# Layer 0 of a four-layer network: 64x64 quadrants for the queries and the attention results, and the values' product moved next to the keys' product

## The chip, the cores and the metric

The program runs on one core of one Trainium2 chip. The metric is the device time of one execution in microseconds (us), and less is better. Everything is computed in fp32.

## The reference, cut to what matters

The network has four layers on an input of 2 x 512 x 32 x 32. Only layer 0, a deformable attention with eight heads of 64 channels, is touched by the change. Cut to the steps that the change and the prediction speak of, it computes:

```python
xn = bn(x)
q = gconv1x1(xn, qw)                     # eight groups of 64 channels, each with its own 64x64 matrix
off = conv(q, off_dw_w, stride 4)        # 6x6 depthwise, padded by 1
...                                      # gelu, tanh: 64 sampling positions for each head
kv = grid_sample(xn, positions)
k = gconv1x1(kv, kw)
v = gconv1x1(kv, vw)
bias = mlp(log-distance of each of 1024 queries to each of 64 positions)   # 2 -> 128 -> 128 -> 1
attn = softmax(q k^T / 8 + bias)
out = attn v                             # 1024 queries x 64 channels for each head
x = x + out_w out + out_b                # then an MLP, and layers 1 to 3
```

The costly part is `mlp` of the bias: 2 images x 8 heads x 64 positions x 1024 queries go through a 128 x 128 matrix.

## The kernel before, in words

**Units.** A head of one image is a *unit* `u` (16 of them). Two heads lie in one tile of 128 channels and make a *pair* (8 pairs). Each unit is cut into 8 steps `o` of two halves `jj`: 16 *quads* for each unit, 256 in all. A quad covers four positions of a head against all 1024 queries.

**The work of a quad.** `first_hidden` (L436) makes the first hidden layer on DVE: four instructions of L445, each 128 x 1024, into two tiles `h1` of a pool of four, so that the quad after next waits until the quad before it has been read. `second_hidden` (L456) makes on PE 4 x 2 x 4 products of 128 x 32 weights (L476, four of them side by side in the four column groups), in four PSUM tiles `hp` of two banks each from the pool `ps` (three such tiles, taken in turn). ACT evicts each `hp` with a ReLU (L481) and scales some (L483, L487), POOL scales and adds (L485, L492, L494) and issues accumulating DMAs (L468). `last_product` (L498, L508) folds two finished quads into `sim`. Every second quad starts with one DVE instruction that makes the table `y` in the PSUM tile `bank` (L433).

**The work behind the quads.** Two generators are advanced by one step after each quad. `front` is `offsets` (L257) and `sampled` (L326) of the next pair. `after` is `attend` (L516) of a finished unit. Their steps that matter here are these:

- `offsets`: L264 makes `xn`; L271 multiplies it by the queries' weights, two products of 128 x 128 by 128 x 512. The weight tile holds the two heads' 64 x 64 matrices on its diagonal and zeros elsewhere. The result `q` takes one tile of `ps`. L274 copies it on ACT into the middle of a 34 x 34 padded image `qpad`. Then DVE makes the depthwise convolution: six products L278 (three in one step, three in the next) and a reduction L291, and so on to the positions.
- `sampled`: the sampled `kv`, then the keys' product (L379) into `bank`, two DVE instructions that scale the keys (L382), the values' product (L384) into another part of `bank`, and its copies to two halves of `v` on DVE (L386) and ACT (L387).
- `attend`: keys by queries into `sim` (L523), DVE's L531, four transposes (L535), the softmax (L540 to L547, the exponential L543 on ACT), four transposes back (L551), a copy (L555), and the product of the values with the attention (L564): two products of 64 x 64 weights by 64 x 512, one for each half of the queries, with the halves' 64 positions in different rows of the array and the results in the same 64 columns. ACT copies the result, 64 x 1024, to `att` (L567). The last unit has no tile of `ps` left and uses `bank` and `sim`, with one copy on ACT (L569) and one on DVE (L570).

**What sets the order.** PE, ACT, DVE and POOL take their instructions strictly in the order in which this code emits them (`manual_schedule`); nothing is reordered. The waits between the engines come from the tiles that they share. In one turn of the loop the code emits the next quad's `first_hidden`, then this quad's `second_hidden`, then one step of `after`, then one step of `front`.

Of the kernel before, what the change touches and what calls it, by code (L numbers as in the profile page):

```python
# [11 lines left out]
F32 = mybir.dt.float32  # L12
# [6 lines left out]
P = 128  # L19
B, C, H, W = 2, 512, 32, 32  # L20
N = H * W
CT = C // P
NB = N // P
HF = 512
DH = 64
NJ = 64
# [21 lines left out]
class Net:  # L48
# [208 lines left out]
    def offsets(self, m, bt, ps):  # L257

        nc = self.nc
        b, t = divmod(bt, CT)
        xn = m["xn"] = self.fone.tile([P, N], F32, tag="xn", name=f"xn{b}{t}")
        nc.vector.tensor_scalar(xn, self.xs[b][t], self.s1[:, t : t + 1], self.col("bn1_b", t), ALU.mult, ALU.add)  # L264
        qp = m["q"] = self.fpool.tile([P, HP, HP], F32, tag="qpad", name=f"qpad{b}{t}")
        for edge in (qp[:, 0, :], qp[:, HP - 1, :], qp[:, :, 0], qp[:, :, HP - 1]):
            nc.gpsimd.memset(edge, 0.0)
        yield
        q = ps.tile([P, 2, HF], F32, tag="ps", name=f"q{b}{t}")
        for h in range(2):  # L270
            nc.tensor.matmul(  # L271
                q[:, h, :], lhsT=self.l0qkv[:, 0, t, :], rhs=xn[:, h * HF : (h + 1) * HF], start=True, stop=True
            )
        nc.scalar.copy(qp[:, 1 : 1 + H, 1 : 1 + W], q.rearrange("p h (r w) -> p (h r) w", w=W))  # L274
        yield
        prod = self.fone.tile([P, 6, 6, NJ], F32, tag="prod", name=f"prod{b}{t}")
        for ky in range(6):
            nc.vector.tensor_tensor(  # L278
                prod[:, ky, :, :].rearrange("p k (y x) -> p k y x", y=8),
                bass.AP(  # L280
                    tensor=qp.tensor,
                    offset=qp[:, ky, 0:1].offset,
                    ap=[list(qp.ap[0]), [1, 6], [4 * HP, 8], [4, 8]],
                ),
                self.colr("dw_w", len(TAPS))[:, 6 * ky : 6 * ky + 6].unsqueeze(2).unsqueeze(3).to_broadcast([P, 6, 8, 8]),
                ALU.mult,
            )
            if ky % 3 == 2:
                yield
        conv = self.fpool.tile([P, NJ], F32, tag="conv", name=f"conv{b}{t}")  # L290
        nc.vector.tensor_reduce(conv, prod.rearrange("p a b j -> p j (a b)"), AX.X, ALU.add)  # L291
        yield
        ge = self.fpool.tile([P, NJ], F32, tag="ge", name=f"ge{b}{t}")
        nc.scalar.activation(ge, conv, AF.Gelu, bias=self.col("dw_b"))
        yield
        o = self.bank[:, 256:258]
        for par in range(2):
            rows = slice(par * DH, (par + 1) * DH)
            nc.tensor.matmul(o[rows, :], lhsT=ge[rows, :], rhs=self.colr("pw", 2)[rows, :], start=True, stop=True)
        at = self.fpool.tile([P, 2], F32, tag="at", name=f"at{b}{t}")  # L300
        nc.scalar.activation(at, o, AF.Tanh)
        yield
        nc.vector.scalar_tensor_tensor(at, at, 4.0, self.grid[:, G_KEY : G_KEY + 2], ALU.mult, ALU.add)
        nc.vector.tensor_scalar(at, at, 2.0 / 7.0, -1.0, ALU.mult, ALU.add)
        pos = self.fpool.tile([P, 2, W], F32, tag="pos", name=f"pos{b}{t}")
        nc.vector.tensor_tensor(
            pos,
            self.grid[:, G_QRY : G_QRY + W].unsqueeze(1).to_broadcast([P, 2, W]),
            at.unsqueeze(2).to_broadcast([P, 2, W]),
            ALU.subtract,  # L310
        )
        yield
        log = self.fpool.tile([P, 2, W], F32, tag="log", name=f"log{b}{t}")
        nc.scalar.activation(log, pos, AF.Abs)
        nc.scalar.activation(log, log, AF.Ln, bias=1.0)
        nc.scalar.activation(pos, pos, AF.Sign)
        yield
        nc.vector.tensor_tensor(log, log, pos, ALU.mult)
        logs = self.dram.tile([P, 2 * W], F32, tag="logs", name=f"logs{b}{t}")
        nc.sync.dma_start(logs, log.rearrange("p d x -> p (d x)"))  # L320
        spots = self.dram.tile([P, 2], F32, tag="spots", name=f"spots{b}{t}")
        nc.sync.dma_start(spots, at)
        m["log"], m["logs"], m["spots"] = log, logs, spots
        yield

    def sampled(self, m, bt, ps):  # L326
# [3 lines left out]
        nc = self.nc  # L330
        b, t = divmod(bt, CT)
        xn = m["xn"]
        g = self.fone.tile([P, 2, 2 * NJ], F32, tag="g", name=f"g{b}{t}")
# [12 lines left out]
        w = self.fone.tile([P, NB, 2 * NJ], F32, tag="w", name=f"w{b}{t}")  # L346
# [16 lines left out]
        for n in range(NB):  # L363
            for par in range(2):
                rows = slice(par * DH, (par + 1) * DH)
                nc.tensor.matmul(
                    kv_ps[rows, :],
                    lhsT=xnT[:, n, rows],
                    rhs=w[:, n, rows],
                    start=(n == 0),  # L370
                    stop=(n == NB - 1),
# [5 lines left out]
        yield  # L377
        k_ps = self.bank[:, 448:512]
        nc.tensor.matmul(k_ps, lhsT=self.l0qkv[:, 1, t, :], rhs=kv, start=True, stop=True)  # L379
        for par in range(2):  # L380
            rows = slice(par * DH, (par + 1) * DH)
            nc.vector.tensor_scalar(keys[rows, par, :], k_ps[rows, :], DH**-0.5, None, ALU.mult)  # L382
        v_ps = self.bank[0:NJ, 256:384]
        nc.tensor.matmul(v_ps, lhsT=kv, rhs=self.l0qkv[:, 2, t, :], start=True, stop=True)  # L384
        vals = self.fpool.tile([P, P], F32, tag="v", name=f"v{b}{t}")
        nc.vector.tensor_copy(vals[0:NJ, :], v_ps)  # L386
        nc.scalar.copy(vals[NJ:P, :], v_ps)  # L387
# [128 lines left out]
    def attend(self, u, m, sim, att, ps):  # L516
        nc = self.nc
        g = u % 8
        rows = slice((g % 2) * DH, (g % 2 + 1) * DH)
        for h in range(2):  # L520
            for jj in range(2):
                at = h * NJ + jj * 32
                nc.tensor.matmul(  # L523
                    sim[at : at + 32, :],
                    lhsT=m["k"][:, g % 2, jj * 32 : jj * 32 + 32],
                    rhs=m["q"][:, 1 + 16 * h : 17 + 16 * h, 1 : 1 + W],
                    start=False,
                    stop=True,
                )
        ss = self.soft.tile([P, HF], F32, tag="ss", name=f"ss{u}")  # L530
        nc.vector.tensor_scalar(ss, sim, self.col("cpb_b3"), None, ALU.add)  # L531
        yield
        tp = ps.tile([P, 8, NJ], F32, tag="ps", name=f"tp{u}") if ps else self.bank.rearrange("p (a j) -> p a j", j=NJ)
        for i in range(4):
            nc.tensor.transpose(  # L535
                tp[:, 2 * i : 2 * i + 2, :].rearrange("p a j -> p (a j)"), ss[:, i * P : (i + 1) * P], self.ident
            )
        st = self.soft.tile([P, 3, 8], F32, tag="st", name=f"st{u}")
        e = self.soft.tile([P, 8, NJ], F32, tag="e", name=f"e{u}")
        nc.vector.tensor_reduce(st[:, 0, :], tp, AX.X, ALU.max)  # L540
        nc.vector.tensor_tensor(e, tp, st[:, 0, :].unsqueeze(2).to_broadcast([P, 8, NJ]), ALU.subtract)
        yield
        nc.scalar.activation(e, e, AF.Exp)  # L543
        yield
        nc.vector.tensor_reduce(st[:, 1, :], e, AX.X, ALU.add)
        nc.vector.reciprocal(st[:, 2, :], st[:, 1, :])
        nc.vector.tensor_tensor(e, e, st[:, 2, :].unsqueeze(2).to_broadcast([P, 8, NJ]), ALU.mult)  # L547
        yield
        pp = ps.tile([P, HF], F32, tag="ps", name=f"pp{u}") if ps else self.bank
        for i in range(4):  # L550
            nc.tensor.transpose(  # L551
                pp[:, i * P : (i + 1) * P], e[:, 2 * i : 2 * i + 2, :].rearrange("p a j -> p (a j)"), self.ident
            )
        pt = self.soft.tile([P, HF], F32, tag="pt", name=f"pt{u}")
        nc.vector.tensor_copy(pt, pp)  # L555
        yield
        if ps:
            o = ps.tile([P, N], F32, tag="ps", name=f"o{u}")
            parts = [o[:, h * HF : (h + 1) * HF] for h in range(2)]
        else:  # L560
            parts = [self.bank, sim]
        for h, part in enumerate(parts):
            half = slice(h * NJ, (h + 1) * NJ)
            nc.tensor.matmul(part[rows, :], lhsT=m["v"][half, rows], rhs=pt[half, :], start=True, stop=True)  # L564
        to = att[g // 2]
        if ps:
            nc.scalar.copy(to[rows, :], o[rows, :])  # L567
        else:
            nc.scalar.copy(to[rows, 0:HF], self.bank[rows, :])  # L569
            nc.vector.tensor_copy(to[rows, HF:N], sim[rows, :])  # L570
        yield

    def project(self, ps, att, w, bias: str, b: int):
# [652 lines left out]
```

## Time and profile before

| | |
|---|---|
| time, three runs | 3575.72, 3578.60, 3578.97 us; median 3578.6 |
| the profiled execution | 3578.05 us, span of its instructions 3576.3 us |
| PE busy | 3497.6 us of the span |
| DVE, ACT, POOL busy | 2023.0, 1976.3, 1869.8 us |
| layer 0 | the first 2106 us, of which the first 36 us are a start without quads |
| L476, all quads | 16384 records in 1825.1 us |

An fp32 product shows as two records of PE, and a record's end is modelled. Four records of different quadrants or column groups run side by side, so that a quad's 64 records take 16 places of 0.43 us. A busy PE therefore does not say that PE never waits: while one column group waits for its data, the records around it still count as busy. The chain of waits shows such places better. In the views that follow, the first number of a timeline or chain row is its start in us, the second how long it lasts.

### The profile page before, as it was taken

Reading aid. Unit: us, or ns where it says so; the run is one execution under the profiler, and the core shown is the slowest. Engines: PE = TensorE matmul, PEld = TensorE weight load, DVE = VectorE, ACT = ScalarE, POOL = GpSimd, SP = SyncE. Lnnn points to the kernel's source line nnn. Section 1 sums busy time; section 2 is a strip of 40 time slices with the busy share of each in tenths; the row PEclk is TensorE's granted clock in tenths of the full one; section 3 lists DMA queues with packets and bytes.
Section 4 is the critical chain, followed back from the end, with each engine's and each line's share of the span. In section 5 each row is a group of like instructions: output and inputs, shape, how many; then the busy total and the mean of one; then the engine's idle time right before and its main releaser. Section 6 shows DMA issues by size and latency. Waiting matters only on the chain.

```text
span 3576.3 us, 58840 instructions
## 1 busy us (share of the span) xinstructions
PE 3497.6 (98%) x25184; PEld 1248.3 (35%) x25184; DVE 2023.0 (57%) x2075; ACT 1976.3 (55%) x2003; POOL 1869.8 (52%) x1392
## 2 busy tenths in 40 slices
PE   7999999999999999999999999999999999999998
PEld 2322332332323332332333334444644333443333
DVE  6877777767767668768766620000242467423674
ACT  5877787877776677777777720011010465102661
POOL 4878777787786687887788810000011344012441
PEclk9999999999999999999999999999999999999999
DMA  5777777787786687787888740000000000000001
GB/s 154 152 144 154 153 152 146 151 162 144 153 160 120 125 161 145 151 159 145 167 163 161 146 162 0 0 0 0 1 3 0 36 1 3 15 0 1 1 1 48
DMA packets 101799, 334.70 MB, mean 94 GB/s; under 512 B 12561, under 2 KB 14225, under 8 KB 100241
## 3 DMA queue, kind: packets, MB, share of 16 engines
q0 software_dynamic: 73296, 266.90, 39.4%
q1 hardware_dynamic: 27216, 61.82, 5.6%
q8 instruction: 202, 3.31, 0.4%
q10 hardware_dynamic: 1008, 2.06, 0.2%
q14 instruction: 77, 0.62, 0.1%
HBM read 59.40 MB, written 4.46 MB: 18 GB/s over the span
## 4 chain that ended last, share of the span: by engine, by line
PE 94%; DVE 5%; issue 1%; ACT 0%; POOL 0%; DMA 0%; DVEq 0%; ACTq 0%
PE hp L476 47%; PE m L619 6%; PE m L628 6%; PE s L956 6%; PE o L985 6%; PE qk0p L848 3%; PE pb L585 3%; PE qk1p L848 3%; PE sim L508 3%; PE vp L889 3%; DVE h L445 2%; DVE prod L278 1%; PE out_b L585 1%; PE d L1002 1%; DVE conv L291 1%; PE ob L193 1%
## 5 line engine op out<-in xcount | busy, mean ns | idle before, releaser
L476 PE MATMUL hp<-h,w 128*32 128x512 f32 x16384 | 1825.1, 593 | 7.4 <-DVE h L445 5.9
L445 DVE CUSTOM_DVE_ANT_1 h<-tx,bank 128x1024 f32<-128x1024 f32 x1024 | 1180.9, 1215 | 344.8 <-PE hp L476 321.7
L481 ACT ACTIVATE h<-hp,magb 128x1024 f32<-128x1024 f32 x1024 | 1123.7, 1112 | 437.1 <-PE hp L476 436.1
L476 PEld LDWEIGHTS hp<-h,w 128*32 128x32 f32 x16384 | 529.6, 110 | 1233.2 <-issue 1151.6
L468 POOL DMA_DIRECT2D h<-h x509 | 452.7, 1026 | 406.7 <-ACT h L487 348.5
L494 POOL TENSOR_TENSOR h<-h,h 128x1024 f32<-128x1024 f32 x255 | 614.6, 2410 | 21.3
L492 POOL TENSOR_SCALAR h<-h,flip 128x1024 f32<-128x1024 f32 x256 | 448.9, 1754 | 0.9 <-ACT h L481 0.9
L960 ACT ACTIVATE e<-s 128x1024 f32<-128x1024 f32 x256 | 258.7, 1024 | 152.7 <-PE s L956 152.6
L483 ACT ACTIVATE h<-h,flip 128x1024 f32<-128x1024 f32 x256 | 291.3, 1138 | 0.0
L956 PE MATMUL s<-q,k 64*64 64x512 f32 x2048 | 259.9, 590 | 5.1 <-ACT e L960 3.4
L985 PE MATMUL o<-e,v 64*64 64x512 f32 x2048 | 260.8, 592 | 0.0
L659 POOL MEMSET l1ones<- 128x128 f32 x1 | 0.2, 205 | 476.0 <-PE m L628 476.0
L623 ACT ACTIVATE mh<-m,cols 128x512 f32<-128x512 f32 x64 | 44.0, 687 | 336.5 <-PE m L619 336.5
L619 PE MATMUL m<-mx,w 128*128 128x512 f32 x512 | 220.5, 592 | 0.9 <-issue 0.9
L628 PE MATMUL m<-mh,w 128*128 128x512 f32 x512 | 220.4, 592 | 0.0
L967 POOL TENSOR_TENSOR some<-some,e 128x1024 f32<-128x1024 f32 x64 | 151.3, 2364 | 82.5 <-ACT e L960 80.0
L636 DVE SCALAR_TENSOR_TENSOR x<-m,cols,x 128x512 f32<-128x512 f32 x16 | 12.0, 750 | 318.0 <-PE m L628 318.0
L485 POOL TENSOR_SCALAR h<-h,flip 128x1024 f32<-128x1024 f32 x128 | 154.5, 1207 | 64.0 <-ACT h L481 62.8
L965 POOL TENSOR_TENSOR some<-e,e 128x1024 f32<-128x1024 f32 x32 | 75.9, 2371 | 212.6 <-ACT q L994 139.2
L862 POOL TENSOR_TENSOR sq<-q 128x1024 f32<-128x1024 f32 x16 | 30.3, 1894 | 280.3 <-DVE q L856 280.3
L860 ACT ACTIVATE k<-qk1p,cols 128x512 f32<-128x512 f32 x32 | 22.0, 687 | 245.0 <-PE qk1p L848 245.0
L487 ACT ACTIVATE h<-h,flip 128x1024 f32<-128x1024 f32 x128 | 145.6, 1138 | 0.0
(206 smaller groups left out, 2708.0 us busy)
## 6 DMA issues: line engine op xcount, KB each, us to landing
h<-h POOLq DMA_DIRECT2D x509, 512.0 KB, 6.5
lb<-logs SPq DMA_DIRECT2D x63, 512.0 KB, 5.2
w<-in_mlp_w SPq DMA_DIRECT2D x8, 1024.0 KB, 11.7
qkv<-in_l_qkv SPq DMA_DIRECT2D x8, 768.0 KB, 5.7
x<-in_x SPq DMA_DIRECT2D x8, 512.0 KB, 9.6
out<-x SPq DMA_DIRECT2D x8, 512.0 KB, 2.6
proj<-in_l_proj SPq DMA_DIRECT2D x8, 256.0 KB, 5.9
l1w<-in_l_w SPq DMA_DIRECT2D x1, 1280.0 KB, 8.2
```

What stands on the lines that cost most here:

```text
L445: self.nc.vector._custom_dve(TENSOR_ADD_SAT, out=h[:, k, :, :], in0=x[:, jj, 2 * r + k, :].unsqueeze(1).to_broadcast([P, H, W]), in1=y[:, ...
L468: nc.gpsimd.dma_start(to, what, accum_op=ALU.add)
L476: nc.tensor.matmul(hp[rows, cut], lhsT=self.l0w2[:, 32 * q : 32 * q + 32], rhs=h1[k][:, cut], start=True, stop=True)
L481: nc.scalar.activation(y, hp, AF.Relu, bias=self.magb[:, q : q + 1])
L483: nc.scalar.activation(ys[0], ys[0], AF.Copy, scale=self.flip[:, 0:1])
L492: nc.gpsimd.tensor_scalar(y, y, self.flip[:, 2:3], 1.0, ALU.mult, ALU.mult)
L494: (nc.vector if final else nc.gpsimd).tensor_tensor(y, y, ys[2], ALU.add)
L619: nc.tensor.matmul(acc, lhsT=w1[t][:, o * P : (o + 1) * P], rhs=xn[t], start=(t == 0), stop=(t == CT - 1))
L628: nc.tensor.matmul(acc, lhsT=w2[t // 4][:, t % 4, o * P : (o + 1) * P], rhs=hs[t], start=(t == 0), stop=(t == nh - 1),)
L956: nc.tensor.matmul(s[halves[c], par, :], lhsT=ks[p][rows, at : at + DH], rhs=qs[p][rows, cut], start=True, stop=True)
L960: nc.scalar.activation(e, s, AF.Exp)
L985: nc.tensor.matmul(o[halves[par], r, :], lhsT=v[rows, n, at : at + DH], rhs=e[rows, par, :], start=(n == 0), stop=(n == NB - 1),)
```

## The change

Three places of layer 0 change; layers 1 to 3, the DMAs and POOL keep their instructions and their order.

1. **Queries.** The two products of 128 x 128 weights become four of 64 x 64, one for each head and each half of the queries, in the four quadrants of the array: the head picks the rows and the PSUM bank, the half of the queries picks the columns. The half of head 0 and that of head 1 therefore lie in swapped partitions, and one ACT copy of 128 x 1024 becomes four copies of 64 x 512: two on ACT, two on DVE.
2. **Attention results.** The two products of 64 x 64 weights by 512 queries become four by 256 queries, again in four quadrants. One ACT copy of 64 x 1024 becomes two of 64 x 512. In the last unit two copies of 64 x 512 become four of 64 x 256.
3. **Values.** The values' product is emitted right after the keys' product, ahead of the scaling of the keys.

```diff
-        for h in range(2):
-            nc.tensor.matmul(
-                q[:, h, :], lhsT=self.l0qkv[:, 0, t, :], rhs=xn[:, h * HF : (h + 1) * HF], start=True, stop=True
-            )
-        nc.scalar.copy(qp[:, 1 : 1 + H, 1 : 1 + W], q.rearrange("p h (r w) -> p (h r) w", w=W))
+        for par in range(2):
+            rows = slice(par * DH, (par + 1) * DH)
+            for h in range(2):
+                nc.tensor.matmul(
+                    q[h * DH : (h + 1) * DH, par, :],
+                    lhsT=self.l0qkv[rows, 0, t, rows],
+                    rhs=xn[rows, h * HF : (h + 1) * HF],
+                    start=True,
+                    stop=True,
+                )
+        for par in range(2):
+            for h in range(2):
+                (nc.scalar.copy if h == par else nc.vector.tensor_copy)(
+                    qp[par * DH : (par + 1) * DH, 1 + 16 * h : 17 + 16 * h, 1 : 1 + W],
+                    q[h * DH : (h + 1) * DH, par, :].rearrange("p (r w) -> p r w", w=W),
+                )
...
         nc.tensor.matmul(k_ps, lhsT=self.l0qkv[:, 1, t, :], rhs=kv, start=True, stop=True)
+        v_ps = self.bank[0:NJ, 256:384]
+        nc.tensor.matmul(v_ps, lhsT=kv, rhs=self.l0qkv[:, 2, t, :], start=True, stop=True)
         for par in range(2):
             rows = slice(par * DH, (par + 1) * DH)
             nc.vector.tensor_scalar(keys[rows, par, :], k_ps[rows, :], DH**-0.5, None, ALU.mult)
-        v_ps = self.bank[0:NJ, 256:384]
-        nc.tensor.matmul(v_ps, lhsT=kv, rhs=self.l0qkv[:, 2, t, :], start=True, stop=True)
...
         if ps:
-            o = ps.tile([P, N], F32, tag="ps", name=f"o{u}")
-            parts = [o[:, h * HF : (h + 1) * HF] for h in range(2)]
+            o = ps.tile([P, 2, HF], F32, tag="ps", name=f"o{u}")
+            parts = [o[:, h, 0 : HF // 2] for h in range(2)]
         else:
-            parts = [self.bank, sim]
+            parts = [self.bank[:, 0 : HF // 2], sim[:, 0 : HF // 2]]
         for h, part in enumerate(parts):
             half = slice(h * NJ, (h + 1) * NJ)
-            nc.tensor.matmul(part[rows, :], lhsT=m["v"][half, rows], rhs=pt[half, :], start=True, stop=True)
-        to = att[g // 2]
-        if ps:
-            nc.scalar.copy(to[rows, :], o[rows, :])
-        else:
-            nc.scalar.copy(to[rows, 0:HF], self.bank[rows, :])
-            nc.vector.tensor_copy(to[rows, HF:N], sim[rows, :])
+            for c in range(2):
+                nc.tensor.matmul(
+                    part[c * DH : (c + 1) * DH, :],
+                    lhsT=m["v"][half, rows],
+                    rhs=pt[half, c * (HF // 2) : (c + 1) * (HF // 2)],
+                    start=True,
+                    stop=True,
+                )
+        to = att[g // 2][rows, :].rearrange("p (h c x) -> p h c x", h=2, c=2)
+        for c in range(2):
+            at = slice(c * DH, (c + 1) * DH)
+            if ps:
+                nc.scalar.copy(to[:, :, c, :], o[at, :, 0 : HF // 2])
+            else:
+                nc.scalar.copy(to[:, 0, c, :], parts[0][at, :])
+                nc.vector.tensor_copy(to[:, 1, c, :], parts[1][at, :])
```

**Waits in the changed program.** The built program shows which instruction waits for which engine. The four copies of the queries form one chain: ACT's first copy waits for PE; DVE's first copy waits for ACT's first; DVE's second follows it; ACT's second waits for DVE's second. The two DVE copies stand in DVE's queue behind the next quad's L445 and ahead of L433 and L445 of the quad after it. The values' product no longer waits for DVE. The copies of the attention results wait for PE alone.

## The prediction

> **What bounds the kernel now.** I read the page first, then the chain of waits in windows around one pair's instructions, then the timelines of DVE and ACT there. The page:
>
> ```profile
> PE 3497.6 (98%) x25184; PEld 1248.3 (35%) x25184; DVE 2023.0 (57%) x2075; ACT 1976.3 (55%) x2003; POOL 1869.8 (52%) x1392
> PE 94%; DVE 5%; issue 1%; ACT 0%; POOL 0%; DMA 0%; DVEq 0%; ACTq 0%
> ```
>
> PE is the chain nearly everywhere, so PE time saved should count, except where the 5% of DVE lies. The chain of waits around the queries of the third pair (columns: start, length) shows where that is:
>
> ```profile
> 579.32 1.91 PE q L271 x4
> 581.23 13.87 PE hp L476 x128
> 595.11 0.86 PE sim L508 x8
> 595.96 0.60 PE pp L551 x4
> ...
> 597.20 6.06 DVE prod L278 x3
> 603.26 0.40 DVE bank L433
> ...
> 603.78 4.62 DVE h L445 x4
> 608.39 4.26 DVE conv L291
> 612.66 4.53 DVE h L445 x4
> ...
> 617.23 7.05 PE hp L476 x58
> ```
>
> PE leads until 596.6; then DVE carries the chain for 20 us, until 617.2. L564, which PE does at 603.5, isn't in it. PE time saved inside this stretch is worth nothing; DVE time lost before it can cost. DVE's and ACT's timelines there:
>
> ```profile
> 578.87 4.62 DVE L445 CUSTOM_DVE_ANT_1 h<-tx,bank 128x1024 f32<-128x1024 f32 x4
> 585.23 2.47 DVE L278 TENSOR_TENSOR prod<-qpad,cols 128x384 f32<-128x384 f32 x3
> 596.59 0.69 DVE L555 COPY pt<-pp 128x512 f32<-128x512 f32 x1 [3.70 <-PE pp L551]
> 580.18 0.63 ACT L543 ACTIVATE e<-e 128x512 f32<-128x512 f32 x1
> 581.27 1.02 ACT L274 COPY qpad<-q 128x1024 f32<-128x1024 f32 x1 [0.46 <-PE q L271]
> ```
>
> DVE's slack before the stretch is the bracket of L555, 3.70 us, and 0.58 us ahead of the L445 at 588.27: 4.3 us. The values, again from the chain:
>
> ```profile
> 442.75 0.21 DVE k L382
> ...
> 443.25 0.43 PE bank L384 x2
> 443.69 7.00 PE hp L476 x64
> ```
>
> PE makes the keys at 441.94 (timeline), then waits behind L531 and both L382 before it makes the values.
>
> **What the Trainium skill says.** "TensorE: Matmul & The Clock Gate", Part 3, says that matmuls in different row and column tiles run concurrently. The trace agrees: in layer 2 a group of eight 64x64 records (L956) starts at 2799.56 and the next at 2800.47, two places of 0.43 us for eight records. "PSUM — Partial Sum Buffer", PSUM bank collisions, says that two engines must not touch one bank and quadrant together, ACT and DVE too. It may be why the four copies are chained; L387 already waits for L386 in this way. "SBUF — State Buffer", Who interferes with whom, says that a DVE instruction with two SBUF inputs and a GpSimd read block each other wholly. The trace agrees: three L278 take 2.47 us at 585.23, 6.06 us at 597.20, where POOL runs L492 and L494.
>
> **Values.** Eight times. From the keys' start to the next quad it is 1.75 us (441.94 to 443.69) for six pairs, 1.42 for the first (83.90 to 85.32) and 1.69 for the second (the gap before its quad, 2.10, less the 0.41 of an ordinary step). Afterwards four small records follow each other unhindered. The nearest row is four transposes of L535, 0.59 us with both changes of tile shape. Saved: 6 x 1.15 + 0.8 + 1.1 = 8.8 us. Bounds: 6.6 us, the idle time in L384's group, and 10.2 us, if the new pair takes only the 0.43 of one product. All is on the path: PE is the chain there, and L445 of the next quad ends 1.7 us before PE wants it, on a DVE that itself loses the 0.52 us wait of L386.
>
> **Attention results.** 15 units by four records in two places of 0.43 us, afterwards eight records in two of 0.215: 0.43 us saved each. In the eight even units L564 is in the chain (481.32, 1.01 us), so 8 x 0.43 = 3.4 us. In the seven odd units it lies in DVE's stretch: 0. Two ACT copies of 0.58 (L569) for one of 1.00 add 0.17 us, after a start 0.43 earlier, ahead of an ACT that then waits for PE. Last unit: 0.43 saved on PE, against two ACT copies of 64x256. A line through 0.58 for 512 and 1.00 for 1024 columns estimates them at 0.38 each, 0.18 more than before: 0.25 saved.
>
> **Queries, on PE.** Four places become two: from 1.91 us to about 1.0 (L564, the same eight-place shape, takes 1.01). It saves 0.91 us in each of seven sites in the loop, if nothing gives it back.
>
> **Queries, the copies.** They do, I think. At the site above, in us after q's start (579.3): ACT's first copy waits for L543, 1.5 to 2.1. DVE, idle since -0.6, is blocked until then: behind the waiting copy are queued L433 and L445 for quad 70, which started at -0.4 before. Two DVE copies of 0.69 (L570), pipelined 1.3 us, end at 3.5; ACT's second ends at 4.2. L433 takes DVE to 4.0, L445 to 8.7 (before 4.2). PE, done with quad 69 at 1.0 + 6.9 = 7.9, gets quad 70's data at 8.7, against its old start of 8.8. The 0.91 us are gone but for 0.1.
> DVE is now 4.5 us late against a slack of 4.3: 0.2 us late at the stretch, if port blocking adds to 8.5 us (2.47 + 6.06) as before. L278's first three move from 5.9 to some 10.4 and meet L492 and L494, the second three then come after POOL's pair: the sum swaps rather than grows. I take 0.2 us lost for six sites: 1.2. (Five are alike. At the sixth, q at 1363.0, L445 for the quad after next ended 2 us later before, but its stretch ends 37.9 us after q too.) Bounds: both threes blocked, +3.6 a site; neither, -3.4.
> ACT is held from 2.1 to 4.2 and frees q's PSUM tile at 4.2; the pool has three tiles, so the third hp of quad 69 wants it, at 1.0 + 2 x 1.7 (two hp of 16 records in four places each) = 4.4: just free. ACT's own lag (0.4 us) meets idle waits of 0.86 and 0.6 us.
> The second pair's site (q at 100.1) has other neighbours. L445 there ends 3.25 us later, and DVE's slack is 1.3 us before quad 12, whose data arrived exactly when PE came (131.17 against 131.18). I price 1.9 less half a us of milder blocking: 1.4 lost (bounds 0.5 and 2).
> Start: q takes 3.79 us for four places at the start's clock, two fewer save 1.72. The copy of 1.03 becomes a chain 0.58 + 1.30 + 0.58 with three handovers of 0.11: 2.79. Net 0 (bounds -0.5 and +0.5).
>
> **Sum.** -8.8 - 3.4 - 0.25 + 1.2 + 1.4 = -9.9 us, on the profiled span 3576.3. That execution took 3578.05, the three runs 3575.7 to 3579.0. From the median 3578.6: **3568.7**.
>
> **Rivals.**
> - *The queries' PE time stays saved.* DVE's blocking falls between the threes and the stretch shortens. For it: 3.7 us of slack and 6 us of blocking there to be lost. Against: DVE arrives late by as much as its slack. With 1.5 us gained at six sites: -9.9 - 1.2 - 9 = -20, 3558.5.
> - *The sum is right in sign but smaller.* The values' pair needs 0.9 us, not 0.6 (-2.4), and each query site loses 0.8 us rather than 0.2 (-3.6): -3.9, 3574.7.
> - *Slower.* The mechanism is DVE's queue at the query copies: both threes of L278 are blocked by POOL, and quad 73 comes 3.6 us later at six sites. 6 x 3.4 more than summed is +20: +10.5, 3589. It passes zero at 9.9 / 6 = 1.7 us a site beyond the 0.2, visible slowness at 2.8. For it: L278 moves straight onto L492. Against: POOL's pair runs once a quad, and to block both threes it must meet DVE twice.
> - *The quadrants don't run together*: against it stands L956.
>
> **Numbers.** Forecast 3568.7 (own range 3564 to 3571): 0.50; queries stay saved: 0.12; smaller: 0.26; slower: 0.12. The bound of 0.2% (what this measurement can tell from no change) is 7.2 us, 3571.4 to 3585.8. Faster 0.62, same 0.26, slower 0.12. The range 3559 to 3580 leaves out the far part of the two outer cases and holds the unknown sizes.
>
> **What would show it.** Right: between keys and hp some 0.6 us; L564 of even units 0.6 us; L271 1.0 us, yet quad 70 starting some 8.7 us after q as before, with DVE's wait ahead of its first copy near 2.8 us; the chain's DVE stretch ending 38 us after q. Wrong: that end moved by over 1 us; ACT or PE waiting for q's tile; the eight records of L271 in more than two places.

## The result and the profile after

The changed kernel takes 3563.35 us (median of six runs, 3562.0 to 3564.75), beside 3576.85 us for the kernel before on the same chip (3575.69 to 3578.97): a ratio of 0.9961, 95% interval 0.9948 to 0.9974, 13.5 us less. That is on the forecast side and in the range, 5.4 us under the forecast of 3568.7 and just under the forecast's own range of 3564 to 3571. Of the 5.4 us, 1.75 lie in the starting point: the forecast set out from the median of three runs, 3578.6, and six runs have 3576.85. The saving is 3.6 us larger than the 9.9 forecast.

The page of the changed kernel, its span, its engines and the shares of its chain:

```profile
span 3561.4 us, 59106 instructions
...
PE 3489.7 (98%) x25280; PEld 1262.1 (35%) x25280; DVE 2028.3 (57%) x2092; ACT 1977.0 (56%) x2027; POOL 1855.6 (52%) x1392
...
PE 90%; DVE 7%; ACT 2%; issue 1%; POOL 0%; DMA 0%; DVEq 0%; ACTq 0%
```

PE has 7.9 us less to do; the span is 14.9 us shorter. But PE's share of the chain fell from 94 to 90% while DVE's rose from 5 to 7% and ACT's from 0 to 2%. Where that sits shows in the chain of waits around the queries of the third pair, the place the prediction showed (start, length, what):

```profile
575.04 2.01 ACT h L492 x2
577.04 0.52 ACT e L554
577.56 0.48 ACT qpad L282
...
578.06 0.69 DVE qpad L282
...
578.77 0.69 DVE qpad L282
579.46 0.40 DVE bank L444
...
579.88 4.62 DVE h L456 x4
...
587.22 4.63 DVE prod L289 x3
...
596.97 2.35 DVE prod L289 x3
...
604.47 4.30 DVE conv L302
608.77 4.53 DVE h L456 x4
...
613.35 7.05 PE hp L487 x58
```

Before, PE led here for 17 us, and only then DVE. Now neither the queries' product nor the quad after it (L487) is in the chain until 613.35: ACT's work before its first copy, the chain of copies, and DVE with all that queues behind them carry it. The same place in DVE's, POOL's and ACT's timelines of the changed kernel (start, length, engine, line, out<-in, shapes, count; in brackets the idle time before and who ended it):

```profile
578.06 1.40 DVE L282 COPY qpad<-q 64x512 f32<-64x512 f32 x2 [3.09 <-ACT qpad L282]
579.38 0.47 DVE L444 TENSOR_SCALAR bank<-lb,cols 128x256 f32<-128x256 f32 x1
...
585.37 1.93 DVE L558 TENSOR_TENSOR e<-e,st 128x512 f32<-128x512 f32 x1
587.22 4.63 DVE L289 TENSOR_TENSOR prod<-qpad,cols 128x384 f32<-128x384 f32 x3
...
596.23 0.74 DVE L566 COPY pt<-pp 128x512 f32<-128x512 f32 x1
596.83 2.49 DVE L289 TENSOR_TENSOR prod<-qpad,cols 128x384 f32<-128x384 f32 x3
...
584.99 1.76 POOL L503 TENSOR_SCALAR h<-h,flip 128x1024 f32<-128x1024 f32 x1
586.83 2.70 POOL L505 TENSOR_TENSOR h<-h,h 128x1024 f32<-128x1024 f32 x1
...
577.45 0.58 ACT L282 COPY qpad<-q 64x512 f32<-64x512 f32 x1
579.49 0.58 ACT L282 COPY qpad<-q 64x512 f32<-64x512 f32 x1 [1.46 <-DVE qpad L282]
```

DVE waits 3.09 us ahead of its first copy (predicted: near 2.8), ACT 1.46 us ahead of its second. L566 is the L555 of before. That one had 3.70 us of idle time ahead of it; L566 has no bracket: DVE's slack is gone. The first three L289 now stand beside POOL's pair L503 and L505 and take 4.63 us; the second three find POOL idle and take 2.49. Before it was 2.47 and 6.06. The other instruction of this step, L558 (e times 1/sum), takes 1.93 us beside POOL, where its L547 took 0.95.

The values, from the chain of the changed kernel, and an even unit's attention results, one line of PE's timeline:

```profile
440.12 0.36 PE bank L390 x2
440.48 0.36 PE bank L392 x2
440.85 7.00 PE hp L487 x64
```

```profile
478.42 0.66 PE L577 MATMUL o<-pt,v 64*64 64x256 f32 x8
```

Keys and values follow each other with nothing between: 0.73 us (440.12 to 440.85), where it was 1.75. The eight records of L577 take 0.6 us of PE's queue (478.42 to 479.01, where L487 follows), where four took 1.01.

**Where the time went.** I lined both traces up at their first query product and compared, quad by quad, where PE ends its last record. A change from one quad to the next is time won or lost in between:

| place | times | after less before, us | predicted |
|---|---|---|---|
| start, to the end of quad 0 | 1 | -1.0 | 0 |
| values | 8 | -7.2 (-0.69, -0.85, six of -0.94) | -8.8 |
| attention results, even units | 8 | -3.3 (-0.41 each) | -3.4 |
| queries of the second pair | 1 | +0.65 (-0.90, then +1.55) | +1.4 |
| queries of six pairs | 6 | -2.6 (four of -0.68 to -0.71, two of +0.10) | +1.2 |
| quad 21 | 1 | -0.3 | not named |
| last unit | 1 | -0.25 | -0.25 |
| all, to the first product of layer 0's last part (L619 before, L640 changed) | | **-14.1** | -9.9 |
| rest of the program, unchanged | | -1.3 | 0 |

What no row names sums to -0.1. The profiled executions differ by 14.9 us (that of the changed kernel also starts its queries 0.56 us later), the medians by 13.5.

Quad 21, which no one had named, is a place where PE's granted clock differs between traces. These are the 10 us around it, in the kernel before and in the later kernel with all copies on ACT (after the busy times of PE, PEld, DVE, ACT and POOL comes the granted clock, then the DMA share and GB/s):

```profile
200.00:210.00 10.00, 7.19 (x79) 2.65 (x75) 8.38 (x9) 4.78 (x6) 6.06 (x6) 0.83 0.73 157
```

```profile
200.00:210.00 10.00, 9.13 (x104) 3.64 (x108) 7.77 (x11) 6.15 (x7) 6.28 (x8) 1.00 0.61 139
```

With a granted clock of 0.83, quad 21 and the 32 small products ahead of it (L366) take 8.31 and 1.46 us in the chain; with 1.00 they take 7.00 and 1.15. The changed kernel has 0.83 too, with 7.46 and 1.97. These 1.3 to 1.6 us come and go between the kernels below, though none of their edits is at quad 21. Why the clock is lower in one and not in the other stays open.

### The profile page after: what moved, and what is told of

Same layout as the page of the kernel before. It is cut to its first block, busy times and chain, and to the rows that moved or that the text cites. A ratio compares the mean times of both kernels' runs of the same rounds, so it can differ in the third digit from the quotient of the medians.

```text
span 3561.4 us, 59106 instructions
## 1 busy us (share of the span) xinstructions
PE 3489.7 (98%) x25280; PEld 1262.1 (35%) x25280; DVE 2028.3 (57%) x2092; ACT 1977.0 (56%) x2027; POOL 1855.6 (52%) x1392
## 4 chain that ended last, share of the span: by engine, by line
PE 90%; DVE 7%; ACT 2%; issue 1%; POOL 0%; DMA 0%; DVEq 0%; ACTq 0%
PE hp L487 45%; PE m L640 6%; PE m L649 6%; PE o L1006 6%; PE s L977 6%; PE pb L606 3%; PE qk0p L869 3%; PE qk1p L869 3%; DVE h L456 3%; PE vp L910 3%; PE sim L519 3%; DVE prod L289 1%; PE out_b L606 1%; PE d L1023 1%; DVE conv L302 1%
## 5 line engine op out<-in xcount | busy, mean ns | idle before, releaser
L487 PE MATMUL hp<-h,w 128*32 128x512 f32 x16384 | 1831.5, 593 | 5.5 <-DVE h L456 3.6
L456 DVE CUSTOM_DVE_ANT_1 h<-tx,bank 128x1024 f32<-128x1024 f32 x1024 | 1180.8, 1216 | 332.5 <-PE hp L487 309.5
L487 PEld LDWEIGHTS hp<-h,w 128*32 128x32 f32 x16384 | 544.1, 110 | 1215.6 <-issue 1120.1
L479 POOL DMA_DIRECT2D h<-h x509 | 451.7, 1024 | 392.9 <-ACT h L498 333.9
L505 POOL TENSOR_TENSOR h<-h,h 128x1024 f32<-128x1024 f32 x255 | 613.6, 2406 | 21.3
L503 POOL TENSOR_SCALAR h<-h,flip 128x1024 f32<-128x1024 f32 x256 | 448.1, 1750 | 0.9 <-ACT h L492 0.9
L640 PE MATMUL m<-mx,w 128*128 128x512 f32 x512 | 220.5, 592 | 0.9 <-issue 0.9
L496 POOL TENSOR_SCALAR h<-h,flip 128x1024 f32<-128x1024 f32 x128 | 145.0, 1133 | 78.5 <-ACT h L492 77.1
```

The lines of the kernel that those rows point to most:

```text
L456: self.nc.vector._custom_dve(TENSOR_ADD_SAT, out=h[:, k, :, :], in0=x[:, jj, 2 * r + k, :].unsqueeze(1).to_broadcast([P, H, W]), in1=y[:, ...
L479: nc.gpsimd.dma_start(to, what, accum_op=ALU.add)
L487: nc.tensor.matmul(hp[rows, cut], lhsT=self.l0w2[:, 32 * q : 32 * q + 32], rhs=h1[k][:, cut], start=True, stop=True)
L503: nc.gpsimd.tensor_scalar(y, y, self.flip[:, 2:3], 1.0, ALU.mult, ALU.mult)
L505: (nc.vector if final else nc.gpsimd).tensor_tensor(y, y, ys[2], ALU.add)
L640: nc.tensor.matmul(acc, lhsT=w1[t][:, o * P : (o + 1) * P], rhs=xn[t], start=(t == 0), stop=(t == CT - 1))
```

## The experiments

Four theories stand in the expectations. **A** is the prediction's: values and attention results bring the gain; the 0.9 us of the queries' product is given back, because DVE waits in its queue for ACT's copy with L444 and L456 behind it, and then meets POOL. **B** says that it is ACT, held by its second copy, that costs. **C** says that the queries' part is itself a good half of the gain. **D** stands for a bound other than DVE: POOL or ACT, or DVE slow by itself. Medians stand beside those of the kernel before on the same chip; "changed" is the changed kernel. A site is the work from one pair's query product to the end of DVE's stretch.

### One part at a time

Queries as before, the rest changed:

```diff
-        for par in range(2):
...
+            nc.tensor.matmul(
+                q[:, h, :], lhsT=self.l0qkv[:, 0, t, :], rhs=xn[:, h * HF : (h + 1) * HF], start=True, stop=True
+            )
+        nc.scalar.copy(qp[:, 1 : 1 + H, 1 : 1 + W], q.rearrange("p h (r w) -> p (h r) w", w=W))
```

> The queries as before (two 128x128 products, one ACT copy), values and attention results as changed. Theory A (the gain is nearly all from values and attention results, a query site gives back most of what PE saves): about 11 us under the kernel before (values 7.2, even attention results 3.3, last unit 0.25), 3 us over the changed kernel; the quads after a query site start where they did before, relative to q. Rival C (the four-quadrant queries are worth their 0.9 us at seven sites): 7.5 us over the changed kernel, 6.5 under the kernel before.

Measured 3567.84 us against 3577.5, ratio 0.9972 (0.9961 to 0.9983): -9.7. Up to the end of the last quad its trace is 10.9 us ahead of the kernel before, where the changed kernel is 13.8 ahead. The work after that quad then takes 2.7 us more, instead of 0.25 less; what that is, is said under the attention results.

The values alone (queries and attention results as before):

> The kernel before with the values' product alone moved. Theory A: 7.2 us under the kernel before, 0.7 at the first pair, 0.85 at the second, 0.94 at six others, the pair of products taking 0.73 us with its change of shape. Rival: the waits that follow on DVE (L433 behind L387) take it back, under 3 us.

Measured 3568.03 against 3576.76, 0.9976 (0.9966 to 0.9987): -8.7. By quads: -0.69, -0.85 and six times -0.94.

The queries alone:

> The kernel before with the queries' part of the change alone. Theory A (DVE decides): 2 to 3 us under the kernel before: quads after a site 0.9 us earlier, then 0.25, then 3.1 late, then 0.7 early or even, the difference being whether POOL's L485 or DVE's third L278 went first in the kernel before; quad 12 0.65 late. Rival C (quadrants are worth 0.9 at seven sites): 6 us or more under.

Measured 3575.26 against 3576.76, 0.9997 (0.9988 to 1.0005): -1.5, not to be told from nothing. A quad after q it is 0.89 ahead, then it gives back 0.64 and 3.4, then it gains 3.04 or 3.83: the pattern of the changed kernel. Quad 21 has a granted clock of 0.66 here (200 to 210 us) against 0.83 before, and comes 1.2 us later. Without that I estimate some -2.7 for the queries' part, still far from C's 6.

The attention results alone:

> The kernel before with the attention results' part of the change alone. Theory A: 0.41 us at each of the eight even units, nothing at the seven odd ones, 0.25 in the last: 3.5 us under the kernel before. Rival (the halves of each copy cost more on ACT than PE saves, or the odd units gain too): 0 or 6.5 us.

Measured 3574.28 against 3576.79, 0.9992 (0.9984 to 1.0001): -2.5. By quads: -0.41 at each even unit, 0 at the odd ones but for shifts of 0.8 either way at six query sites (two of +0.80, four of -0.8), which turn up again below.

The 0.25 us of the last unit don't show here. From the end of the last quad to layer 0's last part this trace is 2.7 us longer than that of the kernel before, and so is the one of the kernel with the queries as before. Two things lie there. PE's last L508 waits for a DMA of POOL: two of its eight records start at 2063.48, the other six at 2064.75. And the granted clock is 0.66 from 2088 to 2093, where one step of L193 (four records) takes 3.69 us in the chain instead of 2.00. Where queries and attention results are both changed, that stretch is 0.25 us shorter, as forecast, in every trace but one (POOL's pair left out). Why it differs stays open, and only one execution was traced. So the -2.5 is a sum of -3.3 from the even units, -1.65 from the shifts and +2.7 at the end, and no clean measure of the part.

The three alone sum to -12.7; a second measurement of the whole (last section of the experiments) gave -11.5, the first -13.5. The sum is close in part by chance: with the attention results alone, the shifts and the late end nearly cancel in it. By quads the parts add up well: the values bring 7.2 us and the even units 3.3, alone as in the whole, and the six query sites 2.5 alone and 2.6 in the whole. The values are the gain, the attention results the smaller part. C fell: the queries alone bring 1.5 us, and the kernel without them keeps 9.7 of the 11.5 to 13.5.

### The copies of the queries, in other hands

All four copies on ACT:

```diff
-                (nc.scalar.copy if h == par else nc.vector.tensor_copy)(
+                nc.scalar.copy(
```

> The changed kernel with all four copies of the queries on ACT, so that DVE's queue has none. Theory A (DVE, held behind the copies, gives the queries' gain back): L456 for the quad after next starts at -0.4 us from q as in the kernel before, quad 70 starts on time, each of the seven sites keeps its 0.9 us up to a race of DVE and POOL worth 0.8; in all some 4 us under the changed kernel, 18 under the kernel before. Rival B (ACT, held until its last copy at 4.2 us after q, is what costs): ACT has 2.1 us of copies in one piece and comes free at 3.7; no more than 1 us from the changed kernel.

Measured 3558.44 against 3577.5, 0.9948 (0.9935 to 0.9962): -19.1, 4.9 under the changed kernel: what A expected (18 and 4), where B allowed 1 us. Its chain of waits at the site:

```profile
572.47 1.02 PE q L273 x8
573.49 13.87 PE hp L487 x128
587.36 0.86 PE sim L519 x8
...
589.45 5.27 DVE prod L289 x3
...
608.68 7.05 PE hp L487 x58
```

PE leads for the first 16 us again, as before the change, with q 0.9 us shorter. Two lines of ACT's and DVE's timelines tell why:

```profile
573.85 2.37 ACT L282 COPY qpad<-q 64x512 f32<-64x512 f32 x4
...
588.85 0.69 DVE L566 COPY pt<-pp 128x512 f32<-128x512 f32 x1 [2.77 <-PE pp L562]
```

ACT makes all four copies in 2.37 us without a gap. DVE no longer has a wait for q, and keeps 2.77 us of slack ahead of L566. For ACT the span from its first copy to its last is much the same as in the changed kernel (2.37 us against 2.62, from 577.45 to 580.07), so this run alone leaves B open; the next but one is made for it.

Against the trace of the changed kernel this one has 2.0 us less at the six sites, 1.6 less at the second pair's and 1.3 less at quad 21. The last is the granted clock named above, 1.00 here and 0.83 there, so not all of the 4.9 us is owed to DVE's queue.

DVE's two copies first, ACT's two after them:

```diff
-        for par in range(2):
-            for h in range(2):
-                (nc.scalar.copy if h == par else nc.vector.tensor_copy)(
+        for copy in (nc.vector.tensor_copy, nc.scalar.copy):
+            for par in range(2):
+                h = par if copy == nc.vector.tensor_copy else 1 - par
+                copy(
```

> The changed kernel with both DVE copies first and both ACT copies after them: DVE waits for PE alone and is free at about 2.5 us after q instead of 3.5, ACT at 3.7 instead of 4.2. Theory A: the quad after next (70) gets its data at 7.7 us and PE isn't held there, 0.65 us less at that quad than in the changed kernel; what comes after depends on where L289 meets POOL, so 0 to 1 us a site, 0 to 6 us in all under the changed kernel. Rival B: 0.5 us of ACT a site changes little, within 1 us of the changed kernel, and quad 70 stays late.

Measured 3565.26 against 3577.5, 0.9967 (0.9955 to 0.9979): -12.2, the time of the changed kernel. DVE's timeline:

```profile
578.44 1.40 DVE L283 COPY qpad<-q 64x512 f32<-64x512 f32 x2 [2.19 <-PE q L273]
...
585.75 2.59 DVE L559 TENSOR_TENSOR e<-e,st 128x512 f32<-128x512 f32 x1
588.26 4.55 DVE L290 TENSOR_TENSOR prod<-qpad,cols 128x384 f32<-128x384 f32 x3
```

The wait is for PE now, and quad 70 comes about on time, so A was right on the wait. The time as a whole hardly moved all the same: L559 (the changed kernel's L558) takes 2.59 us instead of 1.93, and the first three products 4.55. An earlier DVE runs into POOL earlier. A had left open what the meeting with POOL would cost, 0 to 1 us a site. By quads each site is 0.3 us better than in the changed kernel (1.8 in all), and the start, where this trace reads +0.55 and not -1.0, hides it.

The first head's copies on ACT, the second's on DVE, so that DVE waits for both of ACT's:

```diff
-                (nc.scalar.copy if h == par else nc.vector.tensor_copy)(
+                (nc.scalar.copy if par == 0 else nc.vector.tensor_copy)(
```

> The changed kernel with head 0's copies both on ACT and head 1's both on DVE: ACT is not held by DVE any more and is free at 2.7 us after q instead of 4.2, while DVE starts its copies behind both of ACT's and is free at 4.1 instead of 3.5. Theory A: quad 70 comes 0.6 us later than in the changed kernel; later quads the same or up to 0.6 later: 0 to 4 us over the changed kernel. Rival B: ACT's 1.5 us at seven sites come back in part: 3 us or more under the changed kernel.

Measured 3573.26 against 3577.5, 0.9988 (0.9982 to 0.9995): -4.2, 9.9 over the changed kernel. DVE's and ACT's timelines:

```profile
584.41 1.40 DVE L282 COPY qpad<-q 64x512 f32<-64x512 f32 x2 [3.69 <-ACT qpad L282]
...
583.20 1.18 ACT L282 COPY qpad<-q 64x512 f32<-64x512 f32 x2
```

DVE waits 3.69 us instead of 3.09; ACT is through with its copies at 584.38, with no second wait. By B this kernel should be the faster one, and B fell. A has the sign but not the size: 0.6 us of DVE cost 9.9 us in all. Against the trace of the changed kernel some 3.6 us of that are lost at the six sites (0.6 each) and some 5.6 at the second pair's, where three quads run late one after another (+1.39, +2.94, +1.29). That pile-up at the second pair A had not foreseen.

This kernel also answers a guess of the prediction, that a rule on PSUM banks may be why the copies are chained. Here ACT's two copies read one bank and DVE's two the other, and they write different partitions of `qpad`; DVE waits for ACT all the same. So shared banks are not the reason here. What the copies do share are the tiles `q` and `qpad`; that the wait comes from these is likely and not shown. What two engines would bring without that wait was not tried.

### POOL's part in it

POOL's L503 and L505, which run back to back once a quad, left out, so that the kernel leaves a quarter of the second hidden layer out of the bias:

```diff
-            elif q == 2:
-                nc.gpsimd.tensor_scalar(y, y, self.flip[:, 2:3], 1.0, ALU.mult, ALU.mult)
-            elif q == 3:
-                (nc.vector if final else nc.gpsimd).tensor_tensor(y, y, ys[2], ALU.add)
```

> The changed kernel without POOL's two instructions after the third and fourth eviction of each quad (L503, which flips signs in one quarter of the second hidden layer, and L505, which adds that quarter to another): that quarter is left out of the bias, all other work stays. Theory A (what makes quad 39 and its like 3.4 us late is POOL's pair blocking DVE's instructions with two SBUF inputs, L558 and the first three L289): L558 takes 0.7 us and not 1.9, the first three L289 take 2.5 and not 4.6, quad 39 starts on time, and the six sites get 2 us better each. Rival D (L558 and L289 are slow there by themselves, or DVE's lateness is all the copies' holding): both stay within 0.5 us of 1.9 and 4.6, and quad 39 stays 3 us late.

Measured 3542.86 us in one run, against 3576.79. Its DVE timeline at the site, and its L289 over the whole run (least, median and most ns of one):

```profile
578.39 0.69 DVE L554 TENSOR_TENSOR e<-e,st 128x512 f32<-128x512 f32 x1
579.00 2.41 DVE L289 TENSOR_TENSOR prod<-qpad,cols 128x384 f32<-128x384 f32 x3
...
586.72 2.46 DVE L289 TENSOR_TENSOR prod<-qpad,cols 128x384 f32<-128x384 f32 x3
```

```profile
L289 DVE TENSOR_TENSOR prod<-qpad,cols x48: 814/868/927, 11.9 to 1603.9; 128x384 f32<-128x384 f32 x48
```

In the changed kernel the same row reads:

```profile
L289 DVE TENSOR_TENSOR prod<-qpad,cols x48: 815/881/3014, 12.3 to 1626.8; 128x384 f32<-128x384 f32 x48
```

Without the pair no L289 takes over 0.93 us, and the step in which the changed kernel lost 3.4 us (quads 39, 71 and so on) is won back whole at all six sites. Each site is 3.2 us shorter than in the changed kernel, more than the 2 expected: the 3.4 us are saved, and only 0.2 of them are lost at the next quad. Against the kernel before that is -3.0 or -3.9 a site; the prediction's bound for a site without blocking was -3.4. So the long L289 and L558 are indeed DVE held by these two instructions of POOL; before, that was only read off two neighbouring timelines.

The DVE timelines of one site side by side (quads 69 to 72; us after q's start in the chain, or q's first record plus the 0.07 by which the two differ):

| kernel | end of quad 70's first hidden layer | e times 1/sum | first three | second three begin | second three | stretch ends |
|---|---|---|---|---|---|---|
| before | 4.17 | 0.95 | 2.47 | 17.88 | 6.06 | 37.91 |
| changed | 8.43 | 1.93 | 4.63 | 20.76 | 2.49 | 37.28 |
| all on ACT | 4.17 | 0.94 | 3.19 | 16.98 | 5.27 | 36.21 |
| DVE first | 7.52 | 2.59 | 4.55 | 20.50 | 2.45 | 36.95 |
| by heads | 9.03 | 0.96 | 4.58 | 20.39 | 3.45 | 37.81 |
| pair left out | 8.42 | 0.69 | 2.41 | 17.62 | 2.46 | 34.04 |

The end lies 14.0 us after the second three's end in every row; what differs is when these begin and whether POOL stands beside them. The three columns of DVE work that POOL can hold sum to 9.48 before and 9.05 in the changed kernel, and to 5.56 without the pair. Where all copies are on ACT, the row shows the one site of that trace whose second three are short; at the other five they take 6.05 to 6.07 us.

### Spreading the convolution

If the burst of six products meets POOL, shorter steps might slip through: two products a step for three steps, and the reduction in two halves.

```diff
-            if ky % 3 == 2:
+            if ky % 2 == 1:
                 yield
-        nc.vector.tensor_reduce(conv, prod.rearrange("p a b j -> p j (a b)"), AX.X, ALU.add)
-        yield
+        for js in (slice(0, NJ // 2), slice(NJ // 2, NJ)):
+            nc.vector.tensor_reduce(conv[:, js], prod[:, :, :, js].rearrange("p a b j -> p j (a b)"), AX.X, ALU.add)
+            yield
```

On the changed kernel:

> The changed kernel with the convolution spread over more quads: three steps of two L289 in place of two of three, and the reduction L302 in two halves one quad apart. Theory A: what gives the queries' gain back, and the 5 us of PE waiting that six sites had already, is DVE's load in three following quads; spread, most of it goes: 15 to 30 us under the changed kernel, with some 0.6 us left at quad 70 of each site, where DVE is held by the copies. Rival D (the site is bound by POOL or ACT, and DVE only waits with them): within 5 us of the changed kernel.

Measured 3598.91 against 3576.76, 1.0062 (1.0045 to 1.0078): +22.1. With all four copies on ACT besides:

> The same spreading, and all four copies of the queries on ACT. Theory A: as the run before, and each site keeps its 0.9 us and loses nothing at quad 70: 3 to 8 us under the run before, 20 to 30 under the kernel with the copies on ACT alone. Rival D: within 5 us of the kernel with the copies on ACT alone.

Measured 3586.44 against 3576.76, 1.0026 (1.0015 to 1.0037): +9.7. Both expectations missed by far. In the second kernel's trace the stretch itself did get shorter against the one with the copies on ACT: -1.6 and -1.5 us at two quads of a site. But the two added steps push everything later in the pair two quads on, and the step that makes the sampled values (L369 to L372) now falls where PE needs its results. That kernel's chain there:

```profile
435.95 0.90 PE sim L535 x8
...
436.88 0.75 DVE ss L543
...
438.25 2.42 DVE wx L370
...
443.06 4.62 DVE h L457 x4
```

In the kernel with the copies on ACT PE goes on without a gap here (L534, then L390). In this one the quad after the DVE step comes 5.9 to 7.4 us later at six pairs and 5.3 at the second, and the next two 0.9 each. Some of it is clock again: the granted clock is 0.72 from 446 to 452, where the next quad takes 8.22 us instead of 7.00. Spreading moved the collision from the convolution to the next step; on the cause inside the stretch it says nothing against A.

### Both kernels again, on one chip

The changed kernel:

> The changed kernel once more, on the same chip as the next run, to compare them directly: 13 to 14 us under the kernel before.

Measured 3565.31 (3564.38 to 3568.18), 0.9971 (0.996 to 0.9983): -11.5, less than expected. By quads its trace repeats the first one within 0.1 us, but for the start (-0.2, not -1.0) and 0.3 at quad 21. With all four copies on ACT:

> The changed kernel with all four copies of the queries on ACT once more: 4 to 5 us under the changed kernel, 18 to 19 under the kernel before.

Measured 3558.66 (3557.74 to 3561.87), 0.9952 (0.9939 to 0.9966): -18.1, and 6.65 us under the changed kernel beside it, more than the 4 to 5 expected; the ranges don't touch. Of these, 1.6 are quad 21's clock (1.00 here, 0.83 in the changed kernel).

The two traces of the kernel with its copies on ACT differ at three of the six sites, by 0.8 us each. Here are the second three products at the first of the six, in the earlier and in the later one:

```profile
339.78 6.05 DVE L289 TENSOR_TENSOR prod<-qpad,cols 128x384 f32<-128x384 f32 x3
```

```profile
340.75 5.24 DVE L289 TENSOR_TENSOR prod<-qpad,cols 128x384 f32<-128x384 f32 x3
```

It is the same program at the same place, in another execution and on another chip. So which of DVE and POOL goes first there need not come out alike twice.

One line, then, makes a kernel that beats both: values and attention results as changed, the queries in quadrants, and their copies left to ACT.

## Why the prediction came out nearly right

*Values.* The wait behind both L382 went, on the path, in all eight pairs, as said. The size was off: I took the new pair at 0.59 us, from four transposes of L535; it takes 0.36 twice, 0.73. So six pairs bring 0.94 instead of 1.15, and the sum 7.2 instead of 8.8.

*Attention results.* Right in size and place: -0.41 against -0.43 at the even units, nothing at the odd ones but for the shifts below, both in the whole and alone. The last unit brought its 0.25 in the whole; in the two kernels with the attention results and without the queries' part it did not show.

*Queries on PE.* The eight records take two places (1.02 us), so the quadrants do run together, and each site is 0.9 us ahead at first.

*Queries, the copies.* The mechanism held link by link: DVE waits for ACT's first copy (3.09 us against some 2.8), quad 70's first hidden layer ends 8.43 us after q (8.7), 4.3 us later than before (4.5) against a slack of 4.3, DVE's slack is used up, and POOL's blocking moves from the second three to the first. The term that failed is the +1.2 us for six sites: it is -2.6. It rests on "I take 0.2 us lost", with port blocking that adds to 8.5 us as before and "swaps rather than grows". The six products fell to 7.12 us, and L558, which the sum had left out, grew by 0.98: together 9.05 against 9.48. At four sites the stretch ends about 0.6 us earlier (37.28 against 37.91, and 37.24 in the second measurement), of which 0.43 are this blocking. At the two sites of quads 40 and 104 it does not, since in this trace of the kernel before they were already shorter than the one I took for all. There DVE's third product had got ahead of POOL's L485. DVE's and POOL's timelines of the kernel before, first at such a site, then POOL at the one I had read:

```profile
346.08 5.25 DVE L278 TENSOR_TENSOR prod<-qpad,cols 128x384 f32<-128x384 f32 x3
...
350.29 1.89 POOL L485 TENSOR_SCALAR h<-h,flip 128x1024 f32<-128x1024 f32 x1 [0.41 <-ACT h L481]
...
601.41 1.18 POOL L485 TENSOR_SCALAR h<-h,flip 128x1024 f32<-128x1024 f32 x1 [0.41 <-ACT h L481]
```

With DVE first, POOL takes 1.89 us and the three products 5.25; with POOL first it is 1.18 and 6.06. I called the sites alike and had not compared the length of their products. Which sites are the short ones is not fixed: in the four traces whose query sites are as before (the kernel before, no queries' part, values alone, attention results alone) 11 of 24 are short, and not the same ones. So part of the -2.6 is chance too. With four of six long it is -2.6; by the two sizes, -0.70 at a long site and +0.10 at a short one, I estimate -4.2 had all six been long and +0.6 had all been short. The changed kernel has no such choice: its second three take 2.44 to 2.49 us at all six sites, in both its traces.

*Second pair.* A loss, as said, after a gain of 0.9 us on PE: DVE's L456 carries the chain from 126.09 to 130.7, and quad 12 comes 1.55 us late. Net +0.65 instead of +1.4: the three-product steps there got 0.2 and 1.0 us shorter (2.67 to 2.46, 3.50 to 2.52), more than the half us I allowed.

*Start.* Put at 0, it reads -1.0 at the end of quad 0. No run ties this to the edit: over the experiments that figure lies between -1.1 and +0.55, and is -0.75 with the values alone, where nothing at the start is changed.

The sum: values 1.6 less, second pair 0.75 and six sites 3.8 more, start 1.0 more, and 0.4 at quad 21 and in the rest make -14.1 out of -9.9, to rounding. That the forecast lies so near is in part luck: the values, priced too high, make up for part of the sites, priced too low. The six sites are the term that counts. In the rivals' terms, it lies between the forecast and "the queries' PE time stays saved"; that one's mechanism, a shorter stretch, is there at four sites with 0.6 us of its 1.5. The measurement itself leaves room: the same kernel stood 13.5 and 11.5 us under the one before.

What stays open is whether the order of the copies could be made to miss POOL wholly; what the same DVE lateness would cost with another place for the sampled values; and what the split would be worth if the copies of the two engines did not wait for each other. None of these was tried.

## What to carry to other kernels

When a bounding engine is given less work by splitting its output, price the eviction that the split makes: here 0.9 us of PE a site were worth 0.43 on average with the four copies on two engines that wait for each other, and all of it (0.90, but for shifts of 0.8 either way at three sites) with the copies left on the one engine that had time. A copy placed on an engine whose queue feeds the bound costs its wait plus everything queued behind it; look at what stands behind it before you look at its length. And where two engines hold each other up, a step moved in time changes partners: read each site's durations, not one for all, and a second execution before you call a site's length its own.

## What the runs showed of the hardware

- The Trainium skill, "SBUF — State Buffer", Who interferes with whom, says that a DVE instruction with two SBUF inputs contends with a GpSimd instruction that reads SBUF, and that the ports they share are locked for one of them at a time. With POOL's pair left out the slowest L289 is 0.93 us, where it is 3.01 with it: the runs agree. What I had not expected is that the order in which the two meet can differ from site to site and between two executions of one program, and is worth 0.8 us (6.05 against 5.24 us for three products).
- Four ACT copies of 64x512 in a row take 2.37 us, 0.59 each. The changed kernel's alternating chain of four (0.58, 0.69, 0.69 and 0.58, with the handovers) needs 2.62 us by its timelines (577.45 to 580.07): two engines that wait for each other were no faster than one.
- Two products of new weights and few columns (L390, L392) cost 0.36 us each where they follow each other; four transposes of L546 cost 0.59 together, so the one was no measure for the other.
- PE's granted clock fell to 0.83 over the 10 us around quad 21 in some kernels (0.66 in one) and stayed at 1.00 in others; between 0.83 and 1.00 lie 1.3 to 1.6 us of time.
